# Four layers on one core: where the first loads, the ACT tables and the last residual stand at the layer joints

## The chip, the cores and the metric

The kernel runs on one core of one Trainium2 chip, in one launch. The metric is device microseconds of that launch, the median of three runs. Engines are named as in the profile: PE (matmuls), DVE, ACT and POOL (elementwise work), and SP, which here only issues DMAs. ACT can issue DMAs too, from a queue of its own.

## The reference

The input x is 8 samples of 384 channels by 32 x 32 pixels, fp32. Four layers follow each other, each of the form x = x + f(group norm of x):

```python
x = x + mamba(_gn(x))              # layer 0: in_proj, causal conv, silu, x_proj, softplus, scan, gate, out_proj
x = x + deform_and_squeeze(_gn(x)) # layer 1: three deformable depthwise convs (3x3, 5x5, 7x7 on 128 channels each)
x = x + mamba_mlp(_gn(x))          # layer 2: layer norm, mamba as above, then an MLP
x = x + displace(_gn(x))           # layer 3: shift and a 5x5 filter for each group of 8 channels

def _gn(v, G=32, eps=1e-5):        # 32 groups of 12 channels, over all pixels of a sample
    m, s = mean, var over the group
    return (v - m) / jnp.sqrt(s + eps)
```

The scan of a mamba layer runs over the 1024 pixels of a sample for 768 inner channels with 16 states each. Layer 1 multiplies its result, before the residual is added, by a weight for each channel that comes from the mean and the maximum of the whole sample (`se_weight`): so a sample can be finished only when all of its three groups are.

## The kernel before

Channels lie on the 128 partitions, three groups of 128 (G = 3). Layers 0 and 2 are the function `ssm_layer`, layer 1 is `deform_fast` (with a slow way, `deform_layer`, behind a branch that isn't taken here), and layer 3 is worked into the end of layer 2 (`shift_parts`). Between the layers x goes through DRAM (x1, x2). Each layer opens its own pools of SBUF and PSUM, so that its first transfers wait until the layer before is done with that memory.

**A mamba layer.** A step is half a sample (TS = 512 pixels), so there are 16 steps; a step has 6 x 8 = 48 units of scan (6 blocks of 128 inner channels, 8 pairs of states). In the steady part `plan` puts the preparation of the next step (norm, in_proj, conv, silu, x_proj, softplus) into slots between the scan units of the present one, by hand. The first step of a layer has nothing to hide behind: from line 659 its preparation is written out in a row. That row is what the change works on:

- lines 211 to 238: the vector table `vec` (all small weights), the weights `win`, `wout`, `wx`, `wdt`, the diagonal matrices `diag_d` (layer 0 alone, six small DVE operations), and `na` = -exp(A_log), an exp on ACT and a small DVE operation;
- `norm_load` (257): both halves of the first sample, 768 KB each, into the tile x (two buffers);
- `norm_stats` (264), `gn_finish` (124 to 185): statistics on DVE, then two rounds over PE (`gn_mean`, `gn_mean2`, 9 small matmuls each) with a square on ACT between them (167), then a logarithm and an exp on ACT (181, 182); then `norm_apply` on ACT (270);
- layer 2 alone: a layer norm over channels, `ln_mean` to `ln_affine` (280 to 313), with a logarithm and an exp at 302 and 303;
- for each of six blocks d: `inner` (three matmuls of in_proj), `conv_last` on ACT, `conv` on DVE; then `silu` over all six blocks in one ACT operation (350), and `x_proj` (six matmuls, 356), `x_store` (364), and softplus for two blocks (378 to 403), after which the scan begins (443).

Logarithm, exp, silu and sigmoid live in tables that ACT has to load; ACT_TABLE_LOAD rows in the profile are such loads. `exp_ln` (352) asks for the table that has both exp and logarithm.

**The deformable layer.** `deform_fast` first loads the weights and tables of the three kernel sizes on SP's queue, K = 3, 5, 7 in order (936 to 963; for K = 7 `fir_weights`, 1048, loads seven slices and POOL forms six differences of them), then the small weights (964 to 973). After that a table of slots, filled by `put` in `block_steps`, sets the order: the work of sample b, group g in units, two for each quad of filter taps. `load` (1072) brings a whole sample (1536 KB) into `fxn`; `stats` to `norm` (1076 to 1104) normalise it; `conv` and `offsets` compute the sampling positions of a group, which go to DRAM and come back broadcast (`positions`, 1378).

At a sample's end (1348 to 1356) come `fc1`, `relu`, `fc2`, `branches`, `sigmoid`, and for each of the three groups k `residual(k)`, which loads 512 KB of x into a tile with one buffer, and `scale(k)`, which multiplies, adds and stores from the same tile. So load k + 1 waits for store k. For samples 0 to 6 that lies beside the next sample's work; for sample 7 nothing else is left. After it all engines read a flag and take the branch at line 1735.

**Completion semaphores.** The built program hands its DMAs out over eight completion semaphores that SP's and ACT's queues share, and a DMA first waits until the DMA that held its semaphore before has landed. So at most eight are under way.

Of the kernel before, what the change touches and what calls it, by code (L numbers as in the profile page):

```python
# [8 lines left out]
F32 = mybir.dt.float32  # L9
AF = mybir.ActivationFunctionType  # L10
ALU = mybir.AluOpType
# [80 lines left out]
class Net:  # L92
# [107 lines left out]
    def ssm_layer(self, li, src, dst, shift=None):  # L200
        tc, nc, ins = self.tc, self.nc, self.ins
        mlp = li == 2
        gp_c, gp_add = GP_C[li], GP_ADD[li]
        with ExitStack() as ctx:
            wp = ctx.enter_context(tc.tile_pool(name=f"w{li}", bufs=1))
            p1 = ctx.enter_context(tc.tile_pool(name=f"p1_{li}", bufs=1))
            p2 = ctx.enter_context(tc.tile_pool(name=f"p2_{li}", bufs=2))
            self.mm = ctx.enter_context(tc.tile_pool(name=f"mm{li}", bufs=3, space=PSUM))
            dap = ctx.enter_context(tc.tile_pool(name=f"da{li}", bufs=2, space=PSUM))
            yp = ctx.enter_context(tc.tile_pool(name=f"y{li}", bufs=1, space=PSUM))  # L210
            vec = wp.tile([P, ins[f"vec{li}"].shape[1]], F32, name="vec")
            nc.sync.dma_start(out=vec, in_=ins[f"vec{li}"])
# [4 lines left out]
            if mlp:  # L217
                w1_d = ins["w1"].rearrange("(k p) o -> p k o", p=P)
                w2_d = ins["w2"].rearrange("(k p) o -> p k o", p=P)
                mean_w = wp.tile([P, P], F32, name="mean_w")  # L220
                nc.vector.memset(mean_w, 1.0 / C)
            else:
                win = wp.tile([P, G, 2 * DI], F32, name="win")
                nc.sync.dma_start(out=win, in_=win_d)
                wout = wp.tile([P, ND, C], F32, name="wout")
                nc.sync.dma_start(out=wout, in_=wout_d)
                diag_d = wp.tile([P, ND, P], F32, name="diag_d")
                for j in range(ND):
                    nc.vector.tensor_scalar(
                        diag_d[:, j, :], self.ident, vec[:, V_D + j : V_D + j + 1], None, ALU.mult  # L230
                    )
            nc.sync.dma_start(out=wx, in_=ins[f"wx{li}"].rearrange("(k p) o -> p k o", p=P))
            nc.sync.dma_start(out=wdt, in_=ins[f"wdt{li}"])

            na = wp.tile([P, ND, NS], F32, name="na")
            naf = na.rearrange("p d n -> p (d n)")
            nc.scalar.activation(naf, vec[:, V_A : V_A + ND * NS], AF.Exp)
            nc.vector.tensor_scalar(naf, naf, -1.0, -1e-20, ALU.mult, ALU.min)

            def v(i):  # L240
                return vec[:, i : i + 1]
# [15 lines left out]
            def norm_load(s):  # L257
                s["xl"] = []
                for h in (1, 0) if s["h"] == 0 else (1,):
                    x = p2.tile([P, G, TS], F32, name="x", tag="x")  # L260
                    nc.sync.dma_start(out=x, in_=src(s["b"])[:, :, h * TS : (h + 1) * TS])
                    s["xl"].append(x)
# [85 lines left out]
            def silu(s, d0, d1):  # L348
                u = s["u"][:, d0:d1, :]
                nc.scalar.activation(u, u, AF.Silu)  # L350

            def exp_ln():
                nc.scalar.preload_act_table_set("natural_log_exp_and_others")


            def x_proj(s, k0, k1):
                if k0 == 0:
                    s["ps_x"] = self.psum("ps_x", rows=RB)
                for k in range(k0, k1):
                    nc.tensor.matmul(  # L360
                        s["ps_x"], wx[:, k, :], s["u"][:, k, :], start=(k == 0), stop=(k == ND - 1)
                    )
# [295 lines left out]

            with tc.manual_schedule(engines=ENGINES):
                s = steps[0]  # L660
                norm_load(s)
                for i in range(2):
                    norm_stats(s, i)
                s["gn"] = s["sib"]["gn"] = self.gn_finish(s["gn_st"])
# [4 lines left out]
                for d in range(ND):  # L669
                    inner(s, d)  # L670
                    conv_last(s, d)
                    conv(s, d)
                silu(s, 0, ND)
                x_proj(s, 0, ND)
                x_store(s)
                exp_ln()
                for j in range(2):
                    for fn in (dt_proj, soft_exp, soft_rest, soft_ln, soft_sum):
                        fn(s, j)
# [10 lines left out]
                for i, (s, j, m) in enumerate(units):  # L690
                    c, t = divmod(i, T)
# [44 lines left out]
                if mlp:  # L736
# [3 lines left out]
                    last = len(steps) - 1  # L740
# [184 lines left out]
    def deform_fast(self, src, dst):  # L925
        tc, nc, ins = self.tc, self.nc, self.ins
        with ExitStack() as ctx:
# [2 lines left out]
            self.q2 = ctx.enter_context(tc.tile_pool(name="q2", bufs=2))  # L930
            self.mm = ctx.enter_context(tc.tile_pool(name="mm1", bufs=2, space=PSUM))
            self.win_acc = ctx.enter_context(tc.tile_pool(name="win_acc", bufs=1, space=PSUM))
            self.f = {}
            for g, K in enumerate(KS):
                K2, (n, st, cols) = K * K, CONV[K]
                rows = 2 * K2
                ow = wp.tile([P, K * NFIR if n == 1 else K2, rows if n == 1 else st], F32, name=f"fow{K}")
                ob = wp.tile([P, 1], F32, name=f"fob{K}")
                obk = wp.tile([P, 1], F32, name=f"fobk{K}")
                grid = wp.tile([P, cols], F32, name=f"fgrid{K}")  # L940
                for t in (ob, obk, grid) + ((ow,) if n > 1 else ()):
                    nc.gpsimd.memset(t, 0.0)
                if n == 1:
                    self.fir_weights(ow, ins[f"ow{K}"])
                else:
                    nc.sync.dma_start(out=ow[:, :, :rows], in_=ins[f"ow{K}"])
                for i in range(n):
                    r = slice(i * st, i * st + rows)
                    nc.sync.dma_start(out=ob[r], in_=ins[f"ob{K}"])
                    nc.sync.dma_start(out=obk[r], in_=ins["c_cols"][:rows, Q_K + g : Q_K + g + 1])  # L950
                    nc.sync.dma_start(out=grid[r], in_=ins["c_grid"][:rows, i * cols : (i + 1) * cols])
                if n == 1:
                    nc.gpsimd.tensor_scalar(grid[:rows], grid[:rows], obk[:rows], None, ALU.add)
                nc.vector.tensor_tensor(obk, obk, ob, ALU.add)
                nq = K2 // 4
                wk = wp.tile([P, nq + 1, P], F32, name=f"fwk{K}")
                for t in range(4):
                    nc.sync.dma_start(
                        out=wk[H * t : H * (t + 1), :nq, :],
                        in_=ins[f"dw{K}"][t : 4 * nq : 4, :].partition_broadcast(H),  # L960
                    )
                nc.sync.dma_start(out=wk[:, nq, :], in_=ins[f"dw{K}"][4 * nq, :].partition_broadcast(P))
                self.f[K] = (ow, ob, obk, grid, wk)
            pwt = wp.tile([P, G, P], F32, name="pwt")
            nc.sync.dma_start(out=pwt, in_=ins["pw"].rearrange("g c o -> c g o"))
            pwb = wp.tile([P, G], F32, name="pwb")
            nc.sync.dma_start(out=pwb, in_=ins["pwb"])
            f1 = wp.tile([P, G, RK], F32, name="f1")
            nc.sync.dma_start(out=f1, in_=ins["fc1"].rearrange("(k p) o -> p k o", p=P))
            f2 = wp.tile([RK, C], F32, name="f2")  # L970
            nc.sync.dma_start(out=f2, in_=ins["fc2"])
            self.cell = wp.tile([P, 12], F32, name="cell")
            nc.sync.dma_start(out=self.cell, in_=ins["c_cell"])
# [841 lines left out]
```

## Time and profile before

| what | us |
|---|---|
| median of three runs (9529.09 to 9530.19) | 9529.13 |
| the profiled run's own time | 9527.39 |
| its span | 9525.6 |
| PE busy | 8490.7 (89%) |
| DVE busy | 8122.5 (85%) |
| ACT busy | 6483.0 (68%) |
| POOL busy | 5772.1 (61%) |
| first scan of layer 0 starts at | 80.44 |
| last store of layer 0 is issued at | 3054.62 |
| first scan of layer 2 starts at | 6012.78 |

The profile is one execution. The timeline gives each instruction (or a run of equal ones) as start, duration, engine, line, operation, output and inputs, count, and in brackets the idle time ahead of it with what ended it. SPq and ACTq are DMA issues: their duration is that of the issue, not of the transfer. The windows view gives, for a stretch of time, each engine's busy time, PE's granted clock, the busy share of the 16 DMA engines, and GB/s.

Most of the span is the steady part of a layer, in which two or three engines are busy at once. The three joints are stretches in which they are not: 0 to 80 us, about 3037 to 3145 us, and about 5890 to 6012 us.

### The profile page before, as it was taken

Reading aid. Unit: us, or ns where it says so; the run is one execution under the profiler, and the core shown is the slowest. Engines: PE = TensorE matmul, PEld = TensorE weight load, DVE = VectorE, ACT = ScalarE, POOL = GpSimd, SP = SyncE. Lnnn points to the kernel's source line nnn. Section 1 sums busy time; section 2 is a strip of 40 time slices with the busy share of each in tenths; the row PEclk is TensorE's granted clock in tenths of the full one; section 3 lists DMA queues with packets and bytes.
Section 4 is the critical chain, followed back from the end, with each engine's and each line's share of the span. In section 5 each row is a group of like instructions: output and inputs, shape, how many; then the busy total and the mean of one; then the engine's idle time right before and its main releaser. Section 6 shows DMA issues by size and latency. Waiting matters only on the chain. (4 is left out here: it accounts for less than half of the span.)

```text
span 9525.6 us, 87415 instructions
## 1 busy us (share of the span) xinstructions
PE 8490.7 (89%) x27916; PEld 4507.3 (47%) x27916; DVE 8122.5 (85%) x8887; ACT 6483.0 (68%) x10148; POOL 5772.1 (61%) x3795
## 2 busy tenths in 40 slices
PE   7898888888886899999999997699999999999987
PEld 3333333333332677777777776234343434334333
DVE  6989999999997588778778777799999999999973
ACT  5666666666664677778778777667767777777750
POOL 6888888888887000000000000799999999999974
PEclk8999999999998999999999998799999999999998
DMA  2211211121111233333333333233333333332336
GB/s 72 84 59 46 75 62 52 49 84 56 49 66 52 73 79 87 93 77 89 90 82 86 91 83 86 69 116 94 94 94 89 112 117 98 91 94 90 118 103 126
DMA packets 566095, 791.97 MB, mean 83 GB/s; under 512 B 244274, under 2 KB 397266, under 8 KB 542072
## 3 DMA queue, kind: packets, MB, share of 16 engines
q1 hardware_dynamic: 513400, 779.99, 28.2%
q10 hardware_dynamic: 52224, 6.30, 0.5%
q8 instruction: 223, 3.65, 0.2%
q14 instruction: 248, 2.03, 0.1%
HBM read 716.49 MB, written 69.66 MB: 83 GB/s over the span
## 5 line engine op out<-in xcount | busy, mean ns | idle before, releaser
L433 POOL TENSOR_TENSOR db<-du,bc 128x1024 f32<-128x1024 f32 x1536 | 3611.2, 2356 | 417.3 <-DVE hs L443 229.1
L443 DVE TENSOR_TENSOR_SCAN da<-da,db 128x1024 f32<-128x1024 f32 x1272 | 2912.3, 2290 | 199.9 <-ACT da L428 149.0
L474 PE MATMUL y<-hs,ident 128*128 128x512 f32 x5184 | 2603.3, 638 | 379.3 <-DVE hs L457 240.4
L428 ACT ACTIVATE da<-dt,na 128x512 f32<-128x512 f32 x3072 | 2120.0, 691 | 912.4 <-DVE hs L457 682.1
L401 POOL TENSOR_TENSOR dt<-dt,sp_e 128x512 f32<-128x512 f32 x192 | 244.1, 1271 | 2977.7 <-DVE sp_e L393 2977.7
L474 PEld LDWEIGHTS y<-hs,ident 128*128 128x128 f32 x5184 | 1016.3, 203 | 1865.1 <-issue 1131.3
L1483 PE MATMUL wacc<-fsm,fxk 128*128 128x221 f32 (+34 forms) x10624 | 1659.4, 315 | 95.9 <-DVE fsm L1453 93.3
L1483 PEld LDWEIGHTS wacc<-fsm,fxk 128*128 128x128 f32 x10624 | 1572.2, 195 | 234.3 <-DVE fsm L1453 157.1
L457 DVE TENSOR_TENSOR hs<-da,bc 128x1024 f32<-128x1024 f32 x1272 | 1558.0, 1225 | 115.6 <-PE y L474 11.2
L1453 DVE TENSOR_TENSOR fsm<-fhy,fhx 128x170 f32<-128x170 f32 (+42 forms) x3216 | 1171.0, 429 | 344.0 <-PE wacc L1483 317.0
L1413 ACT ACTIVATE fhy<-fpyx,cell 128x416 f32<-128x416 f32 (+9 forms) x1280 | 645.6, 576 | 386.3 <-DVE fsm L1453 386.3
L1436 DVE TENSOR_TENSOR fxk<-fxt,fwk 128x1024 f32<-128x1024 f32 (+1 forms) x688 | 787.5, 1180 | 10.2 <-ACT fxt L1226 10.2
L443 DVE TENSOR_TENSOR_SCAN hs<-da,db 128x1024 f32<-128x1024 f32 x264 | 602.4, 2282 | 71.2 <-POOL db L421 30.0
L454 POOL TENSOR_TENSOR hs<-hs,bc 128x1024 f32<-128x1024 f32 x264 | 622.2, 2357 | 36.6 <-ACT st L449 36.4
L461 POOL TENSOR_TENSOR hs<-hs 128x512 f32<-128x512 f32 x480 | 609.4, 1270 | 3.5 <-DVE hs L457 3.5
L557 PE MATMUL ps_m<-hid,wm 128*128 128x512 f32 x1152 | 536.7, 611 | 30.9 <-ACT hid L550 26.0
L535 PE MATMUL ps_h<-t,wm 128*128 128x512 f32 x1152 | 534.5, 601 | 16.6 <-DVE x L564 16.4
L1418 ACT ACTIVATE fhy<-fhy,cols 128x1344 f32<-128x1344 f32 (+10 forms) x368 | 530.9, 1443 | 12.0
L449 ACT COPY st<-da 128x2 f32<-128x2 f32 x624 | 97.9, 157 | 506.5 <-DVE hs L457 505.2
L1135 PE MATMUL ps_off<-fxn,fow 128*98 128x465 f32 (+10 forms) x896 | 386.6, 579 | 0.0
L1400 ACT ACTIVATE fhx<-fpyx,cell 128x544 f32<-128x544 f32 (+8 forms) x640 | 380.1, 667 | 0.0
L557 PEld LDWEIGHTS ps_m<-hid,wm 128*128 128x128 f32 x1152 | 221.3, 195 | 331.9 <-issue 262.6
(203 smaller groups left out, 9864.1 us busy)
## 6 DMA issues: line engine op xcount, KB each, us to landing
bc<-bcd SPq DMA_DIRECT2D x256, 1024.0 KB
fpyx<-fposd SPq DMA_DIRECT2D x640, 256.0 KB
wm<-in_w SPq DMA_DIRECT2D x96, 768.0 KB
x<-x SPq DMA_DIRECT2D x71, 768.0 KB
winr<-in_win SPq DMA_DIRECT2D x192, 192.0 KB
x<-in_x SPq DMA_DIRECT2D x40, 768.0 KB
fpyx<-fposd SPq DMA_DIRECT2D x24, 1024.0 KB
wm<-in_wout SPq DMA_DIRECT2D x48, 384.0 KB
```

The lines of the kernel that those rows point to most:

```text
L428: nc.scalar.activation(da[:, i, :], s["dt", j], AF.Exp, scale=na[:, j, n : n + 1])
L433: nc.gpsimd.tensor_tensor(db, du, s["bc"][m][:, 0], ALU.mult)
L443: nc.vector.tensor_tensor_scan(h1, da1, db1, 0.0, ALU.mult, ALU.add)
L454: nc.gpsimd.tensor_tensor(s["hs", m], s["hs", m], c, ALU.mult)
L457: nc.vector.tensor_tensor(hs, s["da", m], c, ALU.mult)
L461: nc.gpsimd.tensor_tensor(hs[:, 0, :], hs[:, 0, :], hs[:, 1, :], ALU.add)
L474: nc.tensor.matmul(s["y"], self.ident, s["hs", m][:, i, :], start=first and i == 0, stop=k == NU - 1 and i == n - 1,)
L557: nc.tensor.matmul(ps, s["w2"][:, f, o * P : (o + 1) * P], s["hid", q][:, f, :], start=(f == 0), stop=(f == 3))
L1413: nc.scalar.activation(hy[:, at : at + (yb - ya) * W], pyx[:, 0, ya * W : yb * W], AF.Abs, bias=bias)
L1436: nc.vector.tensor_tensor(t[:, :n], x, wk[:, j : j + 1, :].to_broadcast([P, n, P]), ALU.mult)
L1453: nc.vector.tensor_tensor(self.sub(sm, at, [(r * w, n), (w, r), (1, w)]), self.sub(hy, hy_at[by] + xa, [(r * W, n), (W, r), (1, w)]), self ...
L1483: nc.tensor.matmul(a[:, ya - 4 * o : yb - 4 * o, xa:xb], k, self.sub(sm, sm_at[by], [(w, yb - ya), (1, w)]), start=False, stop=False,)
```

## The change

It does eight things.

1. A mamba layer issues the two loads of its first sample ahead of all its weights (on SP's queue), and `vec` goes to ACT's queue.
2. `diag_d` (layer 0) is made on POOL in place of DVE.
3. `na` is made after the first `x_store` (function `states`), and `exp_ln` is called ahead of the first norm.
4. The first step's silu and x_proj run in two halves of three blocks; the first half of silu stands between the fifth and the sixth block.
5. `deform_fast` issues the load of sample 0 first, on SP's queue.
6. Its tables for K = 7 and the small weights go to ACT's queue, beside those for K = 3 and 5 on SP's.
7. The last sample's residual is loaded in one piece of 1536 KB into `fxn`, eight units before its groups are done.
8. The last sample's three `scale` operations stand in one slot, one after the other.

```diff
@@ ssm_layer
+            begin = []
+            for h in (1, 0):
+                x = p2.tile([P, G, TS], F32, name="x", tag="x")
+                nc.sync.dma_start(out=x, in_=src(0)[:, :, h * TS : (h + 1) * TS])
+                begin.append(x)
             vec = wp.tile([P, ins[f"vec{li}"].shape[1]], F32, name="vec")
-            nc.sync.dma_start(out=vec, in_=ins[f"vec{li}"])
+            nc.scalar.dma_start(out=vec, in_=ins[f"vec{li}"])
...
-                    nc.vector.tensor_scalar(
+                    nc.gpsimd.tensor_scalar(
                         diag_d[:, j, :], self.ident, vec[:, V_D + j : V_D + j + 1], None, ALU.mult
...
-            naf = na.rearrange("p d n -> p (d n)")
-            nc.scalar.activation(naf, vec[:, V_A : V_A + ND * NS], AF.Exp)
-            nc.vector.tensor_scalar(naf, naf, -1.0, -1e-20, ALU.mult, ALU.min)
+
+            def states():
+                naf = na.rearrange("p d n -> p (d n)")
+                nc.scalar.activation(naf, vec[:, V_A : V_A + ND * NS], AF.Exp)
+                nc.vector.tensor_scalar(naf, naf, -1.0, -1e-20, ALU.mult, ALU.min)
...
                 s = steps[0]
-                norm_load(s)
+                s["xl"] = begin
+                exp_ln()
...
                     conv(s, d)
-                silu(s, 0, ND)
-                x_proj(s, 0, ND)
+                    if d == ND - 2:
+                        silu(s, 0, ND // 2)
+                x_proj(s, 0, ND // 2)
+                silu(s, ND // 2, ND)
+                x_proj(s, ND // 2, ND)
                 x_store(s)
                 exp_ln()
+                states()
@@ deform_fast
+            self.xn0 = self.q1.tile([P, G, L], F32, name="fxn")
+            nc.sync.dma_start(out=self.xn0, in_=src(0))
...
+                queue = nc.scalar if K == 7 else nc.sync
...
-                    nc.sync.dma_start(out=ob[r], in_=ins[f"ob{K}"])
-                    nc.sync.dma_start(out=obk[r], in_=ins["c_cols"][:rows, Q_K + g : Q_K + g + 1])
-                    nc.sync.dma_start(out=grid[r], in_=ins["c_grid"][:rows, i * cols : (i + 1) * cols])
+                    queue.dma_start(out=ob[r], in_=ins[f"ob{K}"])
+                    queue.dma_start(out=obk[r], in_=ins["c_cols"][:rows, Q_K + g : Q_K + g + 1])
+                    queue.dma_start(out=grid[r], in_=ins["c_grid"][:rows, i * cols : (i + 1) * cols])
...
-            nc.sync.dma_start(out=pwt, in_=ins["pw"].rearrange("g c o -> c g o"))
+            nc.scalar.dma_start(out=pwt, in_=ins["pw"].rearrange("g c o -> c g o"))
...
@@ fir_weights
-            nc.sync.dma_start(out=w[:, :, k, :], in_=v[:, :, x, :])
+            nc.scalar.dma_start(out=w[:, :, k, :], in_=v[:, :, x, :])
...
@@ block_steps
         def load():
+            if b == 0:
+                sample["xn"] = self.xn0
+                return
...
         def residual(k):
+            if b == self.nb - 1:
+                if k == 0:
+                    sample["xl"] = self.q1.tile([P, G, L], F32, name="fxn")
+                    nc.sync.dma_start(out=sample["xl"], in_=src)
+                sample["xr"] = sample["xl"][:, k, :]
+                return
...
-            for k, t in enumerate((5, 10, 13)):
-                put(end + t - 2, "act0", residual, k)
+            last = b == self.nb - 1
+            for k, t in enumerate((5, 5, 5) if last else (5, 10, 13)):
+                if last:
+                    put(end + t if k else end - 8, "dve1", residual, k)
+                else:
+                    put(end + t - 2, "act0", residual, k)
                 put(end + t, "dve1", scale, k)
```

In the built program the order of the other instructions is the same as before, but for these points. In the first joint ACT's queue holds its 20 DMA issues ahead of the square of the norm (167), and DVE's three small additions to `fobk` (954), which stood ahead of the norm's statistics, stand between 162 and 172. `exp_ln` ahead of the norm leaves a table load in layer 0; in layer 2 it leaves none, and the four loads at 181, 182, 302 and 303 stay.

More of the change, by code (lines that the diff above doesn't have):

```diff
@@ L945, in deform_fast @@
                 else:
-                    nc.sync.dma_start(out=ow[:, :, :rows], in_=ins[f"ow{K}"])
+                    queue.dma_start(out=ow[:, :, :rows], in_=ins[f"ow{K}"])
                 for i in range(n):
                     r = slice(i * st, i * st + rows)
-                    nc.sync.dma_start(out=ob[r], in_=ins[f"ob{K}"])
-                    nc.sync.dma_start(out=obk[r], in_=ins["c_cols"][:rows, Q_K + g : Q_K + g + 1])
-                    nc.sync.dma_start(out=grid[r], in_=ins["c_grid"][:rows, i * cols : (i + 1) * cols])
+                    queue.dma_start(out=ob[r], in_=ins[f"ob{K}"])
+                    queue.dma_start(out=obk[r], in_=ins["c_cols"][:rows, Q_K + g : Q_K + g + 1])
+                    queue.dma_start(out=grid[r], in_=ins["c_grid"][:rows, i * cols : (i + 1) * cols])
                 if n == 1:
@@ L957, in deform_fast @@
                 for t in range(4):
-                    nc.sync.dma_start(
+                    queue.dma_start(
                         out=wk[H * t : H * (t + 1), :nq, :],
@@ L961, in deform_fast @@
                     )
-                nc.sync.dma_start(out=wk[:, nq, :], in_=ins[f"dw{K}"][4 * nq, :].partition_broadcast(P))
+                queue.dma_start(out=wk[:, nq, :], in_=ins[f"dw{K}"][4 * nq, :].partition_broadcast(P))
                 self.f[K] = (ow, ob, obk, grid, wk)
             pwt = wp.tile([P, G, P], F32, name="pwt")
-            nc.sync.dma_start(out=pwt, in_=ins["pw"].rearrange("g c o -> c g o"))
+            nc.scalar.dma_start(out=pwt, in_=ins["pw"].rearrange("g c o -> c g o"))
             pwb = wp.tile([P, G], F32, name="pwb")
-            nc.sync.dma_start(out=pwb, in_=ins["pwb"])
+            nc.scalar.dma_start(out=pwb, in_=ins["pwb"])
             f1 = wp.tile([P, G, RK], F32, name="f1")
-            nc.sync.dma_start(out=f1, in_=ins["fc1"].rearrange("(k p) o -> p k o", p=P))
+            nc.scalar.dma_start(out=f1, in_=ins["fc1"].rearrange("(k p) o -> p k o", p=P))
             f2 = wp.tile([RK, C], F32, name="f2")
-            nc.sync.dma_start(out=f2, in_=ins["fc2"])
+            nc.scalar.dma_start(out=f2, in_=ins["fc2"])
             self.cell = wp.tile([P, 12], F32, name="cell")
-            nc.sync.dma_start(out=self.cell, in_=ins["c_cell"])
+            nc.scalar.dma_start(out=self.cell, in_=ins["c_cell"])
             self.zero = wp.tile([P, HL], mybir.dt.bfloat16, name="zero")
```

## The prediction

> **What bounds the kernel now.** I read the page first (slices, busy shares), then windows to find the stretches where no engine is full, then the timeline of each such stretch engine by engine, and last who waits for whom there. In the steady parts the change alters no order, so I hold them at their time. What is left are three joints in which one chain runs and everything else waits for it.
>
> The start, SP's, DVE's, ACT's and PE's timelines:
>
> ```profile
> 1.76 0.42 SPq L212 DMA_DIRECT2D vec<-in_vec  x1
> 2.23 0.43 SPq L224 DMA_DIRECT2D win<-in_win  x1
> ...
> 9.92 25.85 SPq L261 DMA_DIRECT2D x<-in_x  x4
> ```
>
> ```profile
> 17.78 3.85 DVE L268 BATCH_NORM_STATS2 gn_st<-x 128x6 f32<-128x512 f32 x6 [10.97 <-DMA x<-in_x]
> ```
>
> ```profile
> 31.07 1.28 ACT L182 ACT_TABLE_LOAD   x1
> ...
> 53.73 1.28 ACT L350 ACT_TABLE_LOAD   x1 [1.64 <-DVE u L344]
> 55.02 2.76 ACT L350 ACTIVATE u<-u 128x3072 f32<-128x3072 f32 x1
> ```
>
> ```profile
> 57.84 6.87 PE L360 MATMUL ps_x<-u,wx 128*56 128x512 f32 x12 [6.62 <-ACT u L350]
> ```
>
> The samples are issued behind all weights and DVE idles 10.97 us for them. One table load lies between logarithm and exp, one ahead of silu; then PE does all of x_proj after all of silu.
>
> The first joint, DVE and ACT, and two windows with the DMAs (the last two columns: share of 16 engines, GB/s):
>
> ```profile
> 3096.97 3.66 DVE L1080 BATCH_NORM_STATS2 gn_st<-fxn 128x6 f32<-128x512 f32 x6 [3.06 <-DMA fxn<-x]
> ...
> 3109.62 0.16 DVE L172 TENSOR_TENSOR gn_var<-gn_ps,gn_grp 128x3 f32<-128x3 f32 x1 [4.35 <-PE gn_ps L150]
> ```
>
> ```profile
> 3105.36 0.17 ACT L167 ACTIVATE gn_dm<-gn_ps 128x3 f32<-128x3 f32 x1 [74.60 <-DVE gn_ps L162]
> ```
>
> ```profile
> 3082.00:3086.00 4.00, 0.00 (x0) 0.00 (x0) 0.00 (x0) 0.00 (x0) 4.00 (x3) 0.50 1.22 264
> ...
> 3058.00:3098.00 40.00, 0.00 (x0) 0.00 (x0) 1.51 (x5) 0.00 (x0) 15.92 (x20) 0.50 0.81 181
> ```
>
> The square waits for a sample issued behind 50 weight DMAs, which begin at 3058.20.
>
> The second joint, DVE and SP:
>
> ```profile
> 5911.00 1.28 DVE L1294 SCALAR_TENSOR_TENSOR fxr<-fog,se,fxr 128x1024 f32<-128x1024 f32 x1 [7.87 <-DMA fxr<-x]
> 5918.45 1.28 DVE L1294 SCALAR_TENSOR_TENSOR fxr<-fog,se,fxr 128x1024 f32<-128x1024 f32 x1 [6.16 <-DMA fxr<-x]
> 5924.45 0.17 DVE L221 MEMSET mean_w<- 128x128 f32 x1 [4.71 <-SPq L1735]
> ```
>
> ```profile
> 5903.16 0.34 SPq L1295 DMA_DIRECT2D x<-fxr  x1
> ...
> 5919.77 0.32 SPq L1295 DMA_DIRECT2D x<-fxr  x1
> ...
> 5926.62 1.13 SPq L261 DMA_DIRECT2D x<-x  x2
> ```
>
> Three scales of 1.28 us stand behind store, load, store, load; the branch waits for the last store.
>
> **What the Trainium skill says.** "DMA: Bandwidth & Descriptors", section "Issuing engines are not separate DMA queues": DMAs of SP and ACT share 16 engines, and a second issuing engine saves only issue time. The trace agrees: from 3074 to 3094 those engines are at a share of 0.83 to 1.25 with SP alone issuing. So part 6 is worth what the queue idles, not half. "TensorE: Matmul & The Clock Gate", "What's actually happening": after an idle window of about 3.4 us PE falls to half clock. Here x_proj comes after 6.62 idle and its first matmuls start 0.86 us apart, later ones 0.43. "ScalarE: Activation LUTs", "What ACT_TABLE_LOAD costs": 1.283 us for the load and a drain on top; the trace shows 1.28 and no drain of that size (31.07 + 1.28, exp at 32.36), so I use 1.28.
>
> **The start, part by part.** Samples first: gmat, cols and vec (668 KB) are in at 5.10, where ACT's exp of vec begins. Two samples of 786 KB at the 400 GB/s of the windows from 6 to 10 us land at 7.1 and 9.1; DVE's three statistics for each half (1.93) then end at 11.1, and aggregation lets PE start at 11.3 in place of 21.79: 10.5 saved. win, behind them now, is 2.36 MB, in at about 15; the chain needs it at 22, so it stays hidden. diag_d on POOL: the nearest row, a POOL TENSOR_SCALAR of 98x1024 in 2.85, makes six of 128 columns about 2 to 3 us; POOL has nothing until 70 us, so nothing (if PE had to wait for it, 3). vec on ACT's queue: nothing. The table preload takes the 1.28 at 31.07 off the path (that at 26.49 lay beside PE): 1.3. na costs 0.28 on ACT between table and softplus: -0.3.
>
> Halves: the table load and a half silu (1.4) begin at 49.5 and delay the sixth conv_last from 51.25 to 52.25; its conv on DVE ends at 54.65; second half 54.7 to 56.1; last three x_proj pairs from 56.2. PE idled about 1 us twice, so I take them warm: 6 x 0.43 + 0.26, ending at 59.0 against 64.71: 5.7. Were PE cold, 1.7 less.
>
> Sum: 10.5 + 1.3 - 0.3 + 5.7 = 17.2 (14 to 20).
>
> **The first joint.** The sample goes first and its statistics come early: it shares the engines with the first slices of K = 7, lands at about 3067, and 4.0 (statistics, aggregation) + 4.0 (PE) + 0.5 bring DVE's gn_ps to about 3075.5. But ACT now issues 20 DMAs ahead of the square, each waiting for the one that held its semaphore before, on either queue. So the square, and with it PE's second round, waits for nearly all weights: ACT's queue takes the place of the sample's DMA. The transfers come to 0.81 x 40 = 32.4 us of all engines; at a full share of 1.2 that is 27 us, and with 1.8 from first issue to first byte (as at the start of the span) they end at 3087. Some 0.36 MB are still under way when ACT issues its last, 1.5 us of it: the square at about 3086, against 3105.36: 19. gn_var has three fobk additions ahead of it, and the last waits for POOL: fow's six differences (1.53 each, the last two after the last slice at about 3076) and fgrid (2.85) end near 3082, before the square and PE's 4.25; hidden. Bounds: 0, if ACT's issues run on to 3105; 27, if they don't bind and gn_var follows POOL at 3082.5. From gn_var on all is as before, nothing else stands behind these waits.
>
> **The second joint.** Scales at 5901.85, 5903.13, 5904.41, end 5905.7; the last store issues at 5905.7 in place of 5919.77, and the branch follows it by the same 4.7: 14.0 saved (13.5 if the stores queue behind each other). The 1536 KB residual is issued some 45 us earlier beside a DMA share of 0.3, and 8 semaphores last two units: nothing; if it held up the positions, 3 at most. x first: 5924.55 in place of 5926.62, and without 0.3 MB ahead of it: 2.1 to 2.9, I take 2.5. vec is needed at 5965. na wasn't on this path. Table loads: the built program's order of instructions shows that in layer 2 exp_ln leaves none and those at 182 and 303 stay: 0 of 2.6. Halves as above: 5.7 - 0.3.
>
> Sum: 14.0 + 2.5 + 5.4 = 21.9 (18 to 24).
>
> **Sum.** 17.2 + 19 + 21.9 = 58. Against the profiled run's 9527.4 (span 9525.6 and 1.8 around it) that gives 9469; the median lies 1.7 higher: 9471.
>
> **Rivals.** (a) ACT's queue eats the first joint: eight semaphores shared by two queues make each wait for the other's small DMAs, and the square comes at 3105. For it: 30 DMAs of at most some KB, each with its landing time, and SP now waits for the sample's landing at its sixth. Against: large ones fill the gaps. 39 left: 9490. (b) More: the transfers overlap better than the share says, the square comes at 3078, gn_var at 3082.5, and the sample lands at 6 in the start: 27 + 18 + 22 = 67: 9462. (c) Slower: the two queues fall into step, each DMA waiting for the landing of the one before. A landing costs 2.2 (vec issued 5924.55, used 5926.76); 51 x 2.2 = 112, the square at 3170, 65 lost against 39 gained: 9555. It decides from (3105.4 + 39 - 3058.2) / 51 = 1.7 us a DMA; before it is 0.65. (d) The preload in layer 2 does not happen: counted above.
>
> **How the numbers follow.** Forecast 0.62, (a) 0.18, (b) 0.15, (c) 0.03, and 0.02 for something else that takes the gain. About 0.2% (19 us) can be told from no change: faster 0.94, same 0.03, slower 0.03. The range: lows 14 + 14 + 18 = 46, highs 20 + 27 + 24 = 71, with (a) at 39, gives 9458 to 9490.
>
> **What would show it.** DVE's first statistics at 7 us with no wait over 8; no table load between 181 and 182 in layer 0, but both in layer 2; L167 in the first joint released by nothing DVE did, with ACTq issues up to it, at 3086 less the start's gain; three L1294-type scales back to back; x_proj at twice six matmuls with 0.43 each. Wrong: a square within 3 us of DVE's gn_ps (then b), an in_proj waiting for win, or steady parts that change by over 5 us.

## The result and the profile after

The changed kernel takes 9474.62 us (median of 4 runs, 9470.31 to 9480.32), against 9529.11 (9524.17 to 9530.19) for the kernel before in the same comparison: 54.5 us less, ratio 0.9944, 95% interval 0.9927 to 0.9961. The forecast was 9471. The profiled run of the changed kernel is the slowest of its four, 9480.32 with a span of 9478.5, so the two traces differ by 47.1 us and not by 54.5. They split so:

| stretch | before | after | gained | predicted |
|---|---|---|---|---|
| span's start to layer 0's first scan | 80.44 | 64.71 | 15.7 | 17.2 |
| layer 0's last store to gn_var of the first joint | 55.00 | 41.98 | 13.0 | 19 |
| first of the last scales to layer 2's first scan | 110.93 | 90.76 | 20.2 | 21.9 |
| all the rest | 9279.2 | 9281.0 | -1.8 | 0 |

The rest is steady work whose instructions stand in the same order in both kernels. How far it moves by itself can be read from the profiles of all runs below, which leave it alone too: layer 0 from its first scan to its last store takes between 2969.3 and 2977.0 us, layer 1 from gn_var to the eighth sigmoid between 2788.1 and 2795.3 (before 2792.0, after 2795.3). Taken together, the rest lies between 9270.9 and 9284.0 in the fourteen profiles, so a single profile's total is good to some 7 us either way. A joint repeats better: where its code is the same, the first joint and layer 2's stretch repeat within 1.2 us, but the start of the kernel before took 80.44, 81.52 and 83.39 in the three profiles in which nothing of it is edited.

**The start.** DVE's timeline of the changed kernel:

```profile
7.35 3.89 DVE L277 BATCH_NORM_STATS2 gn_st<-x 128x6 f32<-128x512 f32 x6 [7.35 <-DMA x<-in_x]
```

PE's timeline, same kernel:

```profile
11.40 4.00 PE L140 MATMUL gn_ps<-gn_mv,gmat 128*128 128x2 f32 x18 [11.40 <-DVE gn_mv L132]
...
42.18 2.78 PE L369 MATMUL ps_x<-u,wx 128*56 128x512 f32 x6 [1.14 <-ACT u L359]
46.04 2.78 PE L369 MATMUL ps_x<-u,wx 128*56 128x512 f32 x6 [1.08 <-ACT u L359]
```

The first statistics start at 7.35 in place of 17.78 and run through. x_proj, 6.87 us in one group before, is now two groups of six at 2.78, that is 0.46 a row. (A row is one matmul record of the profile; each of these fp32 matmuls leaves two.)

**The first joint.** ACT's timeline:

```profile
3042.22 15.43 ACTq L1071 DMA_DIRECT2D fow<-in_ow  x7
3059.16 0.60 ACTq L967 DMA_DIRECT2D fob<-in_ob  x1
...
3061.74 9.13 ACTq L976 DMA_DIRECT2D fwk<-in_dw  x4
...
3075.86 0.35 ACTq L991 DMA_DIRECT2D cell<-in_c_cell  x1
3076.31 0.17 ACT L167 ACTIVATE gn_dm<-gn_ps 128x3 f32<-128x3 f32 x1 [61.57 <-DMA fwk<-in_dw]
```

DVE's timeline:

```profile
3048.88 3.66 DVE L1101 BATCH_NORM_STATS2 gn_st<-fxn 128x6 f32<-128x512 f32 x6 [10.31 <-DMA fxn<-x]
...
3057.01 0.17 DVE L162 TENSOR_TENSOR gn_ps<-gn_mv,gn_ps 128x3 f32<-128x3 f32 x1
...
3080.58 0.16 DVE L172 TENSOR_TENSOR gn_var<-gn_ps,gn_grp 128x3 f32<-128x3 f32 x1 [9.19 <-PE gn_ps L150]
```

The square needs gn_ps, which DVE has at 3057.01. It runs at 3076.31, right behind ACT's last DMA issue. The bracket names a DMA, but the square reads nothing that a DMA brings: what it waited for is the queue it stands in. The windows of that stretch (share of the 16 DMA engines and GB/s are the last two columns):

```profile
3050.00:3054.00 4.00, 1.20 (x6) 1.23 (x6) 2.79 (x8) 0.00 (x0) 0.00 (x0) 0.50 1.29 254
3054.00:3058.00 4.00, 2.77 (x14) 2.69 (x13) 0.79 (x3) 0.00 (x0) 3.00 (x2) 0.50 0.58 118
...
3066.00:3070.00 4.00, 0.00 (x0) 0.00 (x0) 0.00 (x0) 0.00 (x0) 2.09 (x2) 0.50 0.68 101
...
3042.00:3078.00 36.00, 5.43 (x25) 5.38 (x26) 5.09 (x14) 0.17 (x1) 16.02 (x20) 0.50 0.89 201
```

The share of the DMA engines is near 1.2 in some stretches and half of that in others; the mean is 0.89.

**The second joint.** DVE's timeline:

```profile
5876.10 3.68 DVE L1322 SCALAR_TENSOR_TENSOR fxn<-fog,se,fxn 128x1024 f32<-128x1024 f32 x3 [0.27 <-ACT se L1307]
5885.35 0.17 DVE L227 MEMSET mean_w<- 128x128 f32 x1 [5.57 <-SPq L1767]
5890.98 3.66 DVE L277 BATCH_NORM_STATS2 gn_st<-x 128x6 f32<-128x512 f32 x6 [5.46 <-DMA x<-x]
```

ACT's timeline:

```profile
5899.64 1.28 ACT L181 ACT_TABLE_LOAD   x1
...
5904.22 1.28 ACT L182 ACT_TABLE_LOAD   x1
...
5921.41 1.28 ACT L312 ACT_TABLE_LOAD   x1
```

The three scales stand in a row without a wait, and the table loads of layer 2 are all still there.

### The profile page after: what moved, and what is told of

It is laid out like the page before. It is cut to its first block, busy times and chain, and to the rows that moved or that the text cites. A ratio compares the mean times of both kernels' runs of the same rounds, so it can differ in the third digit from the quotient of the medians.

```text
span 9478.5 us, 87409 instructions
## 1 busy us (share of the span) xinstructions
PE 8496.4 (90%) x27916; PEld 4511.6 (48%) x27916; DVE 8121.2 (86%) x8881; ACT 6479.3 (68%) x10147; POOL 5774.0 (61%) x3801
## 5 line engine op out<-in xcount | busy, mean ns | idle before, releaser
L466 DVE TENSOR_TENSOR hs<-da,bc 128x1024 f32<-128x1024 f32 x1272 | 1557.7, 1225 | 115.5 <-PE y L483 12.1
```

The source lines that it names most:

```text
L466: nc.vector.tensor_tensor(hs, s["da", m], c, ALU.mult)
```

## The experiments

Times below are medians (lowest to highest in brackets), each with its ratio to the kernel before in the same comparison (that kernel's medians were 9527.6 to 9532.7) and its 95% interval; stretches come from the profiled run.

### What holds the square of the first joint

First, part 6 undone: sample 0 stays first, and all weights go back to SP's queue.

```diff
-                queue = nc.scalar if K == 7 else nc.sync
+                queue = nc.sync
...
-            nc.scalar.dma_start(out=pwt, in_=ins["pw"].rearrange("g c o -> c g o"))
+            nc.sync.dma_start(out=pwt, in_=ins["pw"].rearrange("g c o -> c g o"))
...
-            nc.scalar.dma_start(out=w[:, :, k, :], in_=v[:, :, x, :])
+            nc.sync.dma_start(out=w[:, :, k, :], in_=v[:, :, x, :])
```

> The changed kernel with part 6 undone: all weights of layer 1 on SP's queue again, behind sample 0, which stays first. Theory (ACT's queue holds the square): with no DMA issues on ACT the square of the first joint follows DVE's gn_ps within 0.5 us, that is about 8 us after the sample's landing, at about 3057.5 in place of 3076.31; gn_var near 3062 in place of 3080.58, and the joint some 18 us shorter: about 9456. Rival (the transfers bind): the square comes early too, but the convolutions or the positions then wait for weights issued on one queue, and 15 us or more of the 18 are given back before the first se: 9470 or more. Third (the small additions to fobk bind): gn_var stays within 4 us of where it is.

Measured: 9453.26 us (9448.34 to 9465.67), ratio 0.992 (0.9903 to 0.9936). ACT's timeline:

```profile
3057.66 0.17 ACT L167 ACTIVATE gn_dm<-gn_ps 128x3 f32<-128x3 f32 x1 [42.60 <-DVE gn_ps L162]
```

DVE's:

```profile
3057.40 0.17 DVE L162 TENSOR_TENSOR gn_ps<-gn_mv,gn_ps 128x3 f32<-128x3 f32 x1
3061.92 0.16 DVE L172 TENSOR_TENSOR gn_var<-gn_ps,gn_grp 128x3 f32<-128x3 f32 x1 [4.35 <-PE gn_ps L150]
```

Now DVE's gn_ps releases the square, 0.26 us later. The stretch from the last store to gn_var is 23.0 us in place of 42.0, and nothing of the 19 is given back: from gn_var to the first sigmoid it is 429.2 us, 430.4 in the changed kernel. SP's timeline of this version, first and last of the issues:

```profile
3042.50 0.36 SPq L949 DMA_DIRECT2D fxn<-x  x1
...
3079.78 0.34 SPq L991 DMA_DIRECT2D cell<-in_c_cell  x1
```

One queue issues all 51 DMAs within 37.6 us; the two queues of the changed kernel needed 34.0 (3042.19 to 3076.2). So part 6 ends the issues 3.6 us earlier, for transfers that nobody waits for, and pays with 19 us of an engine in the chain. In the built program the additions to fobk also stand behind gn_var here. Whether these held gn_var was asked by moving them alone, with ACT's queue left as it is:

```diff
-                nc.vector.tensor_tensor(obk, obk, ob, ALU.add)
...
+        def bias():
+            nc.vector.tensor_tensor(obk, obk, ob, ALU.add)
+
+        if b == 0:
+            put((-14, -8, -3)[g], "dve1", bias)
```

> The changed kernel with DVE's three additions to fobk moved behind the first norm of layer 1; K = 7 and the small weights stay on ACT's queue. Theory (ACT's queue holds the square): the square stays behind ACT's last DMA issue, near 3076, gn_var within 1 us of 3080.6, and the time is the same, 9470 to 9480. Rival (the additions hold gn_var): gn_var comes 10 us or more earlier and the time is near 9462.

Measured: 9475.17 (9471.94 to 9486.64), ratio 0.9945 (0.9928 to 0.9961). ACT's timeline:

```profile
3069.90 0.35 ACTq L990 DMA_DIRECT2D cell<-in_c_cell  x1
3070.35 0.17 ACT L167 ACTIVATE gn_dm<-gn_ps 128x3 f32<-128x3 f32 x1 [60.21 <-DMA fwk<-in_dw]
```

Layer 0 ended 4.6 us earlier in this execution, but the stretch from its last store to gn_var is 40.6 us. That is 1.4 less than in the changed kernel, little more than the scatter of this stretch (41.8 to 43.0 in four profiles with the same code), and the square again stands right behind the last issue. The additions weren't the wait. Last, the kernel before with part 5 alone:

```diff
+            self.xn0 = self.q1.tile([P, G, L], F32, name="fxn")
+            nc.sync.dma_start(out=self.xn0, in_=src(0))
...
         def load():
+            if b == 0:
+                sample["xn"] = self.xn0
+                return
```

> The kernel before with part 5 alone: sample 0 of layer 1 first, all weights behind it on SP's queue. Theory (part 5 brings the whole gain of the first joint, part 6 takes back what ACT's queue costs): from layer 0's last store to gn_var 23 us in place of 55.0, and the time 32 us below before: 9495 to 9499. Rival (the gain seen with part 6 undone needs other parts of the change too): 42 us or more in that stretch.

Measured: 9495.98 (9490.35 to 9501.36), ratio 0.9966 (0.9954 to 0.9979), 31.6 us less than before. The stretch is 23.3 us in place of 55.0. Part 5 alone is worth 32 us, and part 6 takes 19 of them back.

### The other parts, one at a time on the kernel before

Parts 2 and 3 weren't run alone; what is said of them is read from the traces. The samples ahead of the weights, without parts 2 and 3:

```diff
+            begin = []
+            for h in (1, 0):
+                x = p2.tile([P, G, TS], F32, name="x", tag="x")
+                nc.sync.dma_start(out=x, in_=src(0)[:, :, h * TS : (h + 1) * TS])
+                begin.append(x)
...
-            nc.sync.dma_start(out=vec, in_=ins[f"vec{li}"])
+            nc.scalar.dma_start(out=vec, in_=ins[f"vec{li}"])
...
-                norm_load(s)
+                s["xl"] = begin
```

> The kernel before with the samples ahead of the weights in layers 0 and 2 and vec on ACT's queue (part 1 alone; diag_d stays on DVE and na ahead of the norm). Theory (only the order of the loads counts): first statistics near 7.4 in place of 17.78, layer 2's from the memset of mean_w in 5.6 in place of 7.1: 10.4 + 1.5 = 12, so 9516 to 9520. Rival (parts 2 and 3 are needed for it: diag_d on DVE and the exp of na on ACT wait for vec ahead of the norm): statistics later than 9, 2 to 4 less. Other rival (win, behind the samples, is late for in_proj): part of the 10.4 is lost between xn and in_proj.

Measured: 9517.92 (9510.09 to 9524.02, 20 runs), ratio 0.9988 (0.9981 to 0.9994). DVE's timeline:

```profile
7.54 1.29 DVE L273 BATCH_NORM_STATS2 gn_st<-x 128x6 f32<-128x512 f32 x2 [3.48 <-DMA x<-in_x]
8.74 1.25 DVE L234 TENSOR_SCALAR diag_d<-ident,vec 128x128 f32<-128x128 f32 x6
9.90 2.46 DVE L273 BATCH_NORM_STATS2 gn_st<-x 128x6 f32<-128x512 f32 x4
```

The landing is as expected, but the six small operations for diag_d now lie between the statistics and cost the chain 1.1 us. On POOL, as in part 2, they take 3.51 us beside it. So, by this trace, part 2 is worth 1.1 us, and only together with part 1. From the start to layer 0's first scan this version gains 8.0 us, not 10.4: the rest went to those 1.1 and to 1.2 on PE (in_proj 18.01 us in place of 17.20, x_proj 7.28 in place of 6.87). In layer 2 the loads gain 1.65 us, and a slower in_proj and x_proj take 2.07. The two stretches together are 8.5 us shorter, so that the median's 11.5 meets the expected 12 is in part luck: the rival about diag_d came true with 1.1 us, and the start alone scatters by some 3.

The halves alone:

```diff
-                silu(s, 0, ND)
-                x_proj(s, 0, ND)
+                    if d == ND - 2:
+                        silu(s, 0, ND // 2)
+                x_proj(s, 0, ND // 2)
+                silu(s, ND // 2, ND)
+                x_proj(s, ND // 2, ND)
```

> The kernel before with part 4 alone (silu and x_proj of the first step in two halves, in both mamba layers). Theory (x_proj runs at 0.43 us between starts once half of it lies between the halves of silu, and half a silu leaves the path): from in_proj's start to the copy of x_proj's result 25.0 us in place of 30.7 at the start, and as much less in layer 2: 5.7 x 2 = 11, so 9518 to 9522. Rival (PE stays slow in x_proj): 4.0 x 2 = 8. Third (the sixth conv_last, which now stands behind half a silu and a table load, gives it all back): 0.

Measured: 9516.23 (9509.94 to 9523.45, 20 runs), ratio 0.9986 (0.9979 to 0.9992). PE's timeline of the start:

```profile
53.12 2.78 PE L360 MATMUL ps_x<-u,wx 128*56 128x512 f32 x6 [1.14 <-ACT u L350]
56.97 2.78 PE L360 MATMUL ps_x<-u,wx 128*56 128x512 f32 x6 [1.08 <-ACT u L350]
```

From in_proj's start to the copy of x_proj's result: 24.9 us in place of 30.7, and 25.2 in place of 30.9 in layer 2. 5.8 us for each, 11.6 in all, as the theory has it. By the medians it is 13.2, which agrees within the interval.

The last residual alone (parts 7 and 8):

```diff
         def residual(k):
+            if b == self.nb - 1:
+                if k == 0:
+                    sample["xl"] = self.q1.tile([P, G, L], F32, name="fxn")
+                    nc.sync.dma_start(out=sample["xl"], in_=src)
+                sample["xr"] = sample["xl"][:, k, :]
+                return
...
-            for k, t in enumerate((5, 10, 13)):
-                put(end + t - 2, "act0", residual, k)
+            last = b == self.nb - 1
+            for k, t in enumerate((5, 5, 5) if last else (5, 10, 13)):
+                if last:
+                    put(end + t if k else end - 8, "dve1", residual, k)
+                else:
+                    put(end + t - 2, "act0", residual, k)
```

> The kernel before with parts 7 and 8 alone (last residual in one load, its three scales in a row). Theory: from the first of the last three scales to the memset behind the branch 9.3 us in place of 22.6, nothing else changes: 13.3, so 9515 to 9519. Rival (the 1536 KB load, issued among the broadcasts of the positions, holds up the last sample's work): the eighth sigmoid comes 1 to 3 us later after the seventh than the 282.8 us of before, and that much is given back.

Measured: 9514.88 (9506.21 to 9521.09, 20 runs), ratio 0.9983 (0.9977 to 0.999). From the first of the last scales to the memset it is 9.2 us in place of 22.6. The eighth sigmoid comes 283.8 us after the seventh, 1.0 more than before; but the version with the samples first, which leaves the residual alone, shows 283.7, so this is no sign of the load.

Which of the two parts does it? The changed kernel with the scales in their old slots:

```diff
-            for k, t in enumerate((5, 5, 5) if last else (5, 10, 13)):
+            for k, t in enumerate((5, 10, 13)):
```

> The changed kernel with part 8 undone: the last sample's scales in slots 5, 10 and 13 again; the residual stays one load, eight units ahead. Theory (nothing else is left to issue in those slots, so that the scales wait for nothing but se): the three scales still stand back to back in 3.7 us, from the first of them to the memset 9.3 us, and the time is that of the changed kernel, 9470 to 9480. Rival (the slots between hold work that DVE does first): the stretch grows by that work, up to 13 us.

Measured: 9471.47 (9468.98 to 9479.25), ratio 0.9941 (0.9925 to 0.9958). DVE's timeline:

```profile
5870.88 3.67 DVE L1322 SCALAR_TENSOR_TENSOR fxn<-fog,se,fxn 128x1024 f32<-128x1024 f32 x3 [0.27 <-ACT se L1307]
5879.83 0.17 DVE L227 MEMSET mean_w<- 128x128 f32 x1 [5.28 <-SPq L1767]
```

The scales still stand back to back, and the stretch from the first of them to the memset is 8.9 us, 9.2 with part 8. Part 7, the single early load, is all of it; part 8 changes nothing.

### What the change leaves

In layer 2 the call of exp_ln ahead of the norm emits no load. With a copy of one column on ACT in front of it, it does:

```diff
                 s["xl"] = begin
+                if mlp:
+                    nc.scalar.activation(na[:, 0, :1], self.col(Q_EPS), AF.Copy)
                 exp_ln()
```

> The changed kernel with one copy of a single column on ACT ahead of exp_ln in layer 2. In the built program one table load then stands behind that copy, and those at 181, 182, 311 and 312 are gone. Theory (two of the four loads lay on the path, the other two beside a wait for PE): the time from the first statistics of layer 2 to its in_proj falls by 2 x 1.28 = 2.6 us, and the time with it, to about 9472, which the runs hardly resolve. Rival (all four lie on the path): 5.1 us. Other rival (the one load is late and holds the logarithm): 0.

Measured: 9476.62 (9468.14 to 9480.07), ratio 0.994 (0.9923 to 0.9956): the medians can't tell it from the changed kernel. The trace can: from layer 2's first statistics to its in_proj 31.55 us in place of 33.92. That is 2.4 of the 2.6 expected. PE's waits ahead of ps_mu and of in_proj are each 1.28 us shorter (2.22 and 2.93 in place of 3.50 and 4.21), one table load each.

In all these runs PE is slow in the joints: gn_mean takes 4.0 us there, and in_proj 17.1 to 18.8 where 36 rows at 0.43 would be 15.5. So matmuls on the identity were put ahead of the first norm:

```diff
                 s["xl"] = begin
+                idle = self.psum("idle")
+                for _ in range(48):
+                    nc.tensor.matmul(idle[:, :P], self.ident, self.ident, start=True, stop=True)
```

> The changed kernel with 48 matmuls of 128 x 128 on the identity ahead of the first norm of layers 0 and 2 (their output isn't used). Theory (PE is at its slow pace through the joints because it comes from idling; in_proj's 18.69 and 18.23 us against 36 x 0.43 = 15.5 show it): in_proj falls to 15.5 to 16.5 at the start, each round of gn_mean from 4.0 to some 2 us, and in layer 2 ps_mu and ps_var too; 5 to 7 us at the start and 5 to 11 in layer 2, in all 10 to 18: 9457 to 9465. Rival (the idle gaps of 2 to 4 us within the chain bring the slow pace back): gn_mean faster, the rest as it was, 2 us each, 4 in all. Other rival (the 48 matmuls end late): gn_mean starts later than 11.40 and 5894.9, and the time grows by that.

Measured: 9473.31 (9470.61 to 9479.4), ratio 0.9941 (0.9925 to 0.9958). PE's timeline, layer 2:

```profile
5872.16 12.50 PE L673 MATMUL idle<-ident 128*128 128x128 f32 x96 [5.07 <-DVEq L1770]
5886.22 2.17 PE L140 MATMUL gn_ps<-gn_mv,gmat 128*128 128x2 f32 x18 [1.55 <-DVE gn_mv L132]
5889.20 4.00 PE L150 MATMUL gn_ps<-gn_dm,gmat 128*128 128x1 f32 x18 [0.81 <-ACT gn_dm L167]
5896.70 5.49 PE L292 MATMUL ps_mu<-xn,mean_w 128*128 128x512 f32 x6 [3.50 <-ACT xn L284]
```

Here gn_mean is twice as fast, and the very next round is slow again: in layer 2, which gained 1.9 us, it is the first rival. At the start both happened. The 96 rows held gn_mean up until 13.65, 2.2 us later than in the changed kernel, but there the pace lasted: gn_mean took 2.07, the next round 2.49 and in_proj 17.59 in place of 4.00, 4.00 and 18.69, and the start gained 2.3 us in all.

Then part 6 undone and the copy together, so the changed kernel with these two edits:

```diff
+                if mlp:
+                    nc.scalar.activation(na[:, 0, :1], self.col(Q_EPS), AF.Copy)
...
-                queue = nc.scalar if K == 7 else nc.sync
+                queue = nc.sync
...
```

> The changed kernel with part 6 undone (all weights of layer 1 on SP's queue, behind sample 0) and the copy ahead of exp_ln in layer 2. Theory (both gains are of stretches in which nothing else runs, so they add): 9474.6 - 19 - 2.6 = 9453, with gn_var of the first joint 23 us after layer 0's last store and 87.4 us from the first of the last scales to layer 2's first scan. Rival (one gain meets the other): the time of the kernel with part 6 undone alone, 9453 to 9456, but one of these two stretches as long as in the changed kernel (42 and 90.8 us).

Measured: 9452.56 (9449.2 to 9454.05), ratio 0.992 (0.9906 to 0.9933). The two stretches are 22.7 and 86.6 us: by the trace the gains add. The median alone couldn't tell this from part 6 undone (9453.26). On top of that, matmuls in every wait of PE:

```diff
+                def busy(n):
+                    ps = self.psum("idle")
+                    for _ in range(n):
+                        nc.tensor.matmul(ps[:, :P], self.ident, self.ident, start=True, stop=True)
+
+                busy(60 if mlp else 36)
...
+                mv = self.gn_aggr(s["gn_st"])
+                ps = self.gn_mean(mv)
+                busy(2)
+                grp, dv = self.gn_dev(mv, ps)
+                ps = self.gn_mean2(self.gn_square(dv))
+                busy(9)
+                s["gn"] = s["sib"]["gn"] = self.gn_rstd(grp, self.gn_sum(grp, ps))
...
+                        if fn in (ln_mean, ln_var):
+                            busy(14 if fn is ln_mean else 12)
```

> The best version so far with matmuls of the identity (output not used) in every wait of PE in the first steps of layers 0 and 2: 36 and 60 ahead of the norm, 2 between its rounds, 9 behind them, and in layer 2 14 and 12 around the layer norm. Theory (PE's pace follows how busy it was in the last few us, so filled waits keep it at 0.43 us between starts): gn_mean and gn_mean2 some 2.1 us each in place of 4.0, ps_mu and ps_var 2.6 to 3 in place of 4.4 to 5.5, in_proj 15.5 in place of 17.2 to 18.8; some 6 us at the start and 8 to 10 in layer 2: 9436 to 9439. Rival (the small matmuls of the norm let the pace fall whatever lies around them): gn_mean alone gets faster, 4 us in all: 9449. Other rival (the fillers delay the work behind them): at or above 9452.

Measured: 9440.49 (9434.11 to 9445.6), ratio 0.9907 (0.989 to 0.9923). PE's timeline, layer 2:

```profile
5866.62 2.07 PE L140 MATMUL gn_ps<-gn_mv,gmat 128*128 128x2 f32 x18
...
5869.50 2.17 PE L150 MATMUL gn_ps<-gn_dm,gmat 128*128 128x1 f32 x18 [0.26 <-ACT gn_dm L167]
...
5875.25 2.74 PE L292 MATMUL ps_mu<-xn,mean_w 128*128 128x512 f32 x6
...
5887.26 15.72 PE L333 MATMUL ps_in<-xn,winr 128*128 128x512 f32 x36 [0.26 <-ACT xn L322]
```

In layer 2 every step of the chain is at the fast pace. The clock that the profile says PE was granted agrees: 1.00 over the whole in_proj, and in the changed kernel 0.50 over gn_mean and 0.58 over the first 6 us of in_proj. The last stretch falls from 86.6 to 79.7 us and the first scan of layer 0 comes at 60.88 in place of 64.58: 10.7 in all, under the 14 to 16 expected, in part because gn_mean2 at the start took 3.84. The medians lie 12.1 apart (measured in two comparisons), and the ranges of the two versions don't meet. The same in the first joint:

```diff
+            if b == 0:
+                for slot, count in ((5, 46), (6, 2), (8, 8)):
+                    put(t + slot, "pe1", busy, count)
             put(t + 6, "pe0", mean)
```

> The version with filled waits, with 46, 2 and 8 matmuls of the identity in the first joint too (ahead of the norm of layer 1, between its rounds and behind them; output not used). Theory (the pace of PE is set by what it did in the last few us): gn_mean and gn_mean2 near 2.1 us each in place of 3.97 and 4.00, the first convolution a little shorter, from layer 0's last store to gn_var 19 us in place of 23: 9436. Rival (46 matmuls end too early or too late for the sample's statistics): gn_mean at its slow pace or late, no gain in that stretch, 9440.

Measured: 9437.04 (9435.55 to 9444.87), ratio 0.9904 (0.9888 to 0.9921), and from the last store to gn_var 24.1 us: no gain. PE's timeline:

```profile
3033.33 10.54 PE L1117 MATMUL idle<-ident 128*128 128x128 f32 x92 [0.78 <-DVE x L536]
3048.62 4.00 PE L140 MATMUL gn_ps<-gn_mv,gmat 128*128 128x2 f32 x18 [4.75 <-DVE gn_mv L132]
```

The fillers started right after layer 0, ended at 3043.9, and after 4.75 us of idling gn_mean was at the slow pace: the rival. The start, whose code is that of the version before, had gn_mean2 at 2.51 us this time. The 3.5 us between this median and the one before lie within the spread of the runs, so the version with filled waits in layers 0 and 2 is as good as can be told.

## Why the prediction was right, and where it missed

By its medians the change gained 54.5 of the 58 predicted, but the three priced stretches gained 48.9 in the profiles. The other 5.6 us lie in no term of the working, and nothing in these profiles accounts for them beyond the scatter of single executions. So the mechanisms were right in the main, but part of the closeness to 9471 is luck.

- **Samples first, the start (10.5).** PE's first round at 11.40, predicted 11.3: 10.4 gained. win wasn't missed.
- **Table and na (1.3, -0.3).** From PE's first round to xn 1.28 more; na cost 0.16 between x_proj's result and the scan.
- **Halves (5.7 and 5.4).** From the end of in_proj to x_proj's result 5.7 and 5.8 us less. But in_proj itself took 18.69 and 18.23 us in place of 17.20 and 17.33, which the sum had held constant: -1.5 and -0.9. This is the whole miss of the start. It is no fixed cost of the change: unedited, the start's in_proj took 17.20, 17.49 and 18.59 in three profiles, and with the change 18.04 to 18.80 in six.
- **First joint (19).** The mechanism was right: ACT's queue takes the place of the sample's DMA, and the square runs when ACT's last DMA is issued. The size was off in one term, "at a full share of 1.2 that is 27 us". The issues ran for 34.0 us at a mean share of 0.89; the square came 34.1 us after the first issue and not 27.8. The 6.3 between are the miss, 13.0 for 19. A full share was read from three windows of before (1.19 to 1.25), and windows of 0.15 to 0.83 stood beside them. The waits that rival (a) named are there: from 3064.61 to 3067.91 neither queue issues anything, and the share over 3066 to 3070 is 0.68. They took some of the 19, not all of it. That they make up the whole 6.3 wasn't tested.
- **The fobk additions and POOL.** Hidden, as said; moving the additions alone changes the stretch by 1.4 us, little more than it scatters by.
- **What the working didn't ask.** It priced parts 5 and 6 as one sum. Apart they are +32 and -19, and rival (b)'s 27 was not the most that the joint could give.
- **Tail (14.0).** 13.4. The alternative that it named ("13.5 if the stores queue behind each other") fits the size: the last store was issued as early as computed, but from the end of the last scale to the memset it is 5.57 us in place of 4.72. That the stores before it cause this was not tested.
- **Samples first, layer 2 (2.5).** 1.5. They are issued 0.20 us after the memset in place of 2.17, as computed, but land 5.43 us later in place of 4.94. The gain for "0.3 MB ahead of it" didn't come, and no run shows why.
- **Table loads of layer 2 (0).** All four stayed.
- **Steady parts (0).** -1.8 in the two profiles, within what they scatter.

## What to carry to other kernels

A queue on a compute engine isn't free: in this program each DMA issue there stands in the engine's order, and if it waits for another transfer to land, so does the next arithmetic behind it. Before moving loads to such a queue, find the first instruction behind them and who waits for it; here an operation of 0.17 us, held behind 20 issues, cost 19 us, and putting the needed transfer first was worth more than a second queue. Price each part of a change by itself, since parts with opposite signs hide in a sum. And where a chain of short steps waits by turns, look at PE's time for each row: keeping it busy in its waits was worth 11 us in the trace and 12 by the medians, with work whose result nobody reads.

## What the runs showed of the hardware

**PE's slow stretch has no fixed length.** The same in_proj of 36 rows, after 2 to 4 us of idling, took between 17.10 and 18.80 us in different kernels, layers and executions; with the waits filled it took 15.62, 15.72, 15.72 and once 16.69. Its single rows show where the time goes: at the start of the kernel before, the first four follow each other at 0.58 to 1.01 us, in the changed kernel the first seven at 0.80 to 1.02, and all later ones at 0.43. So the slow pace lasted 3.3 us in one and 6.1 us in the other. The Trainium skill, "TensorE: Matmul & The Clock Gate", section "What's actually happening", has a window of 3413 ns that runs freely and doesn't begin with the kernel; stretches of about one to two such windows agree with it, though no run here shows the windows themselves. So 1.5 us in a joint can come or go without an edit: of the 3.0 us between the shortest and the longest start with the same code (80.44 and 83.39), 2.1 are in_proj and x_proj.

**Filling doesn't hold the pace for certain.** After 12.5 us of fillers and one small round of matmuls (2.17 us, between waits of 1.55 and 0.81) the next round was slow in layer 2 (4.00). At the start of the same kernel, after as many fillers, a round of 2.07 and a wait of 0.73, it was mostly fast (2.49). And the start of the two versions with filled waits, which is the same code, had this round at 3.84 and 2.51. In layer 2 every step was fast in both.

**A second issuing queue helped the transfers little.** With the sample first, 51 DMAs took 37.6 and 39.5 us to issue from one queue (part 6 undone; part 5 alone) and 34.0 from two; the mean share of the DMA engines over the first 36 us is 0.78 with one (part 6 undone) and 0.89 with two. The Trainium skill, "DMA: Bandwidth & Descriptors", section "Issuing engines are not separate DMA queues", says that DMAs of all issuing engines run on the same 16 DMA engines; these times, a tenth apart and not a half, agree.
